# 34 more tiles of gathered rows issued by ScalarE, in one stream of 20 rows a step, with a smaller descriptor store

## Chip, cores and metric

One core of a Trainium2 chip. The metric is device time in microseconds (us) of one execution of the whole kernel; before the change the median of three runs is 10925.68 us (10925.35 to 10929.42).

## What is computed

A recommendation model in fp32, for 16384 users with 69 items each and one label item. The table `emb` has 100001 rows of 96 numbers; the rows are gathered by index, which is most of what the kernel has to move.

```python
u = emb[batch_user]                       # 16384 x 69 x 96
ql = emb[batch_label[:, 0]]               # 16384 x 96
q = jnp.broadcast_to(ql[:, None, :], u.shape)
z = jnp.concatenate([q, u, q - u, q * u], axis=-1)
h = _dice(z @ W1 + b1, a1, EPS_DICE)      # 64 wide
att = (h @ W2 + b2) @ W3 + b3
eff = (batch_user < ITEM_NUM)[..., None]
pre = jnp.where(eff, u * att, 0.0)
pooled = jnp.einsum('gf,bfe->bge', window, pre).reshape(u.shape[0], G * E)
x = jnp.concatenate([pooled, ql], axis=-1)
h = _dice(_bn_eval(x @ Wf1 + bf1, EPS_BN), af1, EPS_DICE)
h = _dice(_bn_eval(h @ Wf2 + bf2, EPS_BN), af2, EPS_DICE)
return h @ Wf3 + bf3
```

`_dice(x, alpha)` is `(alpha * (1 - p) + p) * x` with `p` the sigmoid of the scaled `x`.

## The kernel before

The users are cut into 32 blocks of 512 (`NBLK`, `BLK`). The 512 x 69 rows of a block are 69 chunks (`NCH`) of 512 rows, and a chunk is four tiles (slots 0 to 3) of 128 rows, a row on each partition. The 64 first items of the users make 64 "main" chunks, in which a chunk holds 8 users; the other five items are "tail" chunks of 512 users. Two chunks are a pair, and there are 32 x 69 / 2 = 1104 pairs (`NPAIR`). 1104 x 8 = 8832 tiles of rows are needed, and 128 more for the labels.

There are three ways by which a tile gets into SBUF:

- **GpSimd (POOL)** issues one indirect DMA for a tile: `gather`, line 266 in the trace. It reads 128 indices from `ids` and fetches 128 rows of 384 bytes into the pair's buffer `u` (pool `upool`, 14 buffers, each holding a pair's eight tiles), or into `q` for labels.
- **SyncE (SP)** issues 128 single DMAs of one row each (line 301) for slot 3 of the chunks in `SP_CHUNKS`: the second chunk of every tenth pair, 109 tiles. Its buffers are the first four tiles of `ring`.
- **ScalarE (ACT)** does the same for slot 3 of the chunks in `ACT_CHUNKS`: the first chunk of every eighth pair, 136 tiles, in the next three tiles of `ring`.

For single rows the engine needs each row's place in a register. `Singles.load` (line 286) fetches 32 offsets from the tile `offsets` to registers with one load instruction; then every row is a register move and a DMA issue. Offsets are row numbers times 384, made once at the start by two DVE operations. A tile of rows counts as here when its semaphore reaches 16 x 128; PE waits for that before it transposes the tile (`wait_for_single`).

The order of the work on each engine is written out by hand (`tc.manual_schedule`): `plan` is a list of work for each step, a step for each pair, and the engines' queues get their instructions in that order. In step i stand, in this order: the attention logits of four pairs every fourth step (`attend_rows`: PE `prow`, then the ScalarE copy `row`), the tail chunks of pair i-3, the logits' spreading (`spread`), the hidden layer of pair i-2 (`hidden`: PE `ph`, then on ScalarE the sigmoid of line 405 and the scaling of line 406, then DVE's product `y`), ScalarE's rows of this step (`scalar_rows`), the pooling of pair i-7 (`pool`: PE `acc`, the last use of that pair's tiles in `u` or `ring`), and the fetch of pair i (`fetch`: eight gathers or fewer on POOL, eight transposes `ptr` on PE, two copies and two products on DVE). Every 34.5 steps a block's label rows, its `As` rows (ScalarE copies of `pc`, line 349) and its top layers (lines 483 and 484 on ScalarE) come in between.

ScalarE's rows of one tile are spread over eight steps, 16 rows in each (`ACT_ROWS`, `ACT_STEPS`): tile s is fetched in steps 8s+1 to 8s+8 and used in pair 8s+11. POOL's queue holds nothing but gathers; before the first gather of a pair it waits until the pair 14 before has been pooled. [...]

Of the kernel before, what the change touches and what calls it, by code (L numbers as in the profile page):

```python
# [18 lines left out]
P = 128  # L19
# [31 lines left out]
SLOT = 3  # L51
SP_CHUNKS = [2 * (10 * s + 8) + 1 for s in range(109)]
SP_RING = 4
ACT_CHUNKS = [2 * (8 * s + 11) for s in range(136)]
ACT_RING = 3
ACT_ROWS = 16
ACT_STEPS = -(-P // ACT_ROWS)
SINGLES = SP_CHUNKS + ACT_CHUNKS
NSB = (len(SINGLES) + P - 1) // P
NSEM = 8  # L60


def chunk_of(c):
# [52 lines left out]
def rec_kernel(  # L116
# [12 lines left out]
    nc = tc.nc  # L129
# [1 line left out]

    const = ctx.enter_context(tc.tile_pool(name="const", bufs=1))
    ipool = ctx.enter_context(tc.tile_pool(name="ipool", bufs=2))
    upool = ctx.enter_context(tc.tile_pool(name="upool", bufs=14))
    tpool = ctx.enter_context(tc.tile_pool(name="tpool", bufs=4))
    ypool = ctx.enter_context(tc.tile_pool(name="ypool", bufs=6))
    rpool = ctx.enter_context(tc.tile_pool(name="rpool", bufs=2))
# [137 lines left out]
    class Singles:  # L275

        def __init__(self, name, engine, kind, chunks, first, buffers, group):
            self.name, self.engine, self.kind, self.group = name, engine, kind, group
            self.chunks, self.first, self.buffers = chunks, first, buffers
            self.sems = [tc.alloc_semaphore(f"{name}{k}") for k in range(NSEM)]  # L280
            self.given = [0] * NSEM

# [12 lines left out]
        def fetch(self, s, start, stop):  # L295

            b, k = self.buffers[s % len(self.buffers)], s % NSEM
            for r in range(start, stop):
# [299 lines left out]
    for s, m in enumerate(SP_CHUNKS):  # L598
        at(max(0, m // 2 - 6), lambda s=s: by_sync.fetch(s, 0, P))

    by_scalar = Singles(
        "act",
        nc.scalar,
        mybir.EngineType.Activation,
        ACT_CHUNKS,
        len(SP_CHUNKS),
        range(SP_RING, SP_RING + ACT_RING),
        2 * ACT_ROWS,
    )
    turn = {}  # L610
    for s, m in enumerate(ACT_CHUNKS):
        for k in range(ACT_STEPS):
            turn.setdefault(m // 2 - 2 - ACT_STEPS + k, []).append((s, k * ACT_ROWS, min(P, (k + 1) * ACT_ROWS)))

    def scalar_rows(i):

        for s, start, stop in turn.get(i, []):
            by_scalar.fetch(s, start, stop)

    c = NPAIR - CLOSE  # L620
    for i in range(c):
        if i >= 3 and (i - 3) % 4 == 3:
            at(i, rows_of(i - 6, 4))
        if i >= 3:
            at(i, tails_of(i - 3))
        if i >= 4 and (i - 4) % 4 == 3:
            at(i, spread_of(i - 7, 4))
        if i >= 2:
            at(i, hidden_of(i - 2))
        at(i, lambda i=i: scalar_rows(i))  # L630
        if i < c - CLOSE:
            if i >= POOL_LAG:
                at(i, pool_of(i - POOL_LAG))
        else:

            for k in {0: (-15, -14), 1: (-13,), 3: (-12, -11), 4: (-10, -9), 7: (-8, -7)}.get(i - c + 8, ()):
                at(i, pool_of(c + k))
        at(i, fetch_of(i))
# [116 lines left out]
```

## Time and profile before

| | us |
|---|---|
| median of three runs | 10925.68 |
| the profiled execution | 10926.71 |
| its span, first to last instruction | 10924.9 |
| PE busy (matmuls, their ends modelled) | 8862.0 |
| POOL busy | 8226.3 |
| DVE busy | 4285.5 |
| ScalarE busy, without DMA issue and loads | 1897.5 |
| share of the 16 DMA engines taken by the gathers' queue | 18.7% |

Granted PE clock: 0.745 of full speed in the mean.

How to read it: a line of the groups ("L266 POOL ...") has the line of the code, the engine, the operation, what it writes and reads, how often; behind the bar the busy time of all, the mean of one in ns, then how long the engine stood idle just before them and what ended most of it. "issue" is idle time that ended without the profile showing anything waited for. `ACTq` and `SPq` are the sequencers of ScalarE and SyncE, which issue DMAs and loads; that time is not counted as busy time of the engine. The queue that counts is the one whose idle time nobody else ends.

### The profile page before, as it was taken

How to read it: one execution, taken by the hardware profiler on the slowest of the kernel's cores; microseconds unless marked ns; L12 is line 12 of the kernel's file. 1: busy time of each engine (PE TensorE's matmuls, PEld its weight loads, DVE VectorE, ACT ScalarE, POOL GpSimd, SP SyncE). 2: the span in 40 equal slices, each digit the busy share in tenths (PEclk: the TensorE clock that was granted, in tenths of full speed). 3: DMA queues.
4: the chain of work that ended last, by engine and by line, in shares of the span. 5: the costliest groups of instructions: out<-in, count | busy, mean ns of one | idle time of the engine just before them, and what ended most of it. 6: DMA issues, size and time to landing. Idle time of an engine off the chain costs nothing.

```text
span 10924.9 us, 172203 instructions
## 1 busy us (share of the span) xinstructions
PE 8862.0 (81%) x41797; PEld 4319.5 (40%) x41797; DVE 4285.5 (39%) x7535; ACT 1897.5 (17%) x2761; POOL 8226.3 (75%) x8721
## 2 busy tenths in 40 slices
PE   7878878788887888888878778878888887888878
PEld 3333434343333344333433333334343333433335
DVE  4334333333333333433333333333333333333334
ACT  1111111111111111111111111111111111111112
POOL 7777777777777777777777777777777777777776
PEclk7767777777777777767777777777777777777777
DMA  2212211121111212212111121112212112122111
GB/s 49 42 42 44 42 42 41 42 44 42 42 42 42 44 41 42 42 41 44 42 42 41 42 44 42 42 42 42 44 42 42 42 41 44 42 42 41 42 41 36
DMA packets 344467, 458.51 MB, mean 42 GB/s; under 512 B 202354, under 2 KB 202866, under 8 KB 343330
## 3 DMA queue, kind: packets, MB, share of 16 engines
q0 software_dynamic: 278880, 428.92, 18.7%
q1 hardware_dynamic: 29762, 11.82, 0.5%
q10 hardware_dynamic: 34816, 6.75, 0.4%
q8 instruction: 336, 5.51, 0.2%
q14 instruction: 673, 5.51, 0.2%
HBM read 446.74 MB, written 0.07 MB: 41 GB/s over the span
## 4 chain that ended last, share of the span: by engine, by line
POOL 49%; issue 21%; PE 17%; DMA 12%; DVE 0%; ACT 0%; ACTq 0%; POOLq 0%; DVEq 0%
POOL u L266 48%; DMA u<-in_rows,ids 12%; PE p L502 4%; PE acc L325 4%; PE ph L399 3%; PE ph L403 2%; PE ptr L325 2%; POOL q L266 1%; PE prow L414 1%; PE pa L423 1%; PE ph L396 0%; PE ph L401 0%; PE pc L348 0%; PE patt L431 0%; ACTq L301 0%
## 5 line engine op out<-in xcount | busy, mean ns | idle before, releaser
L266 POOL DMA_INDIRECT u<-in_rows,ids x8587 | 8104.3, 944 | 2620.1 <-issue 2428.2
L325 PE MATMUL ptr<-ident,u 128*96 128x128 f32 x8587 | 2002.8, 332 | 1940.1 <-DMA u<-in_rows,ids 1892.9
L407 DVE TENSOR_TENSOR y<-ph,y 128x512 f32<-128x512 f32 x1104 | 763.5, 692 | 4377.1 <-ACT y L406 4119.6
L325 PEld LDWEIGHTS ptr<-ident,u 128*96 128x96 f32 x8587 | 1139.7, 149 | 2701.4 <-DMA u<-in_rows,ids 2262.6
L325 PEld LDWEIGHTS acc<-rw,u 128*96 128x96 f32 x15930 | 1677.0, 187 | 1204.3 <-issue 977.6
L376 DVE COPY uT<-ptr 96x512 f32<-96x512 f32 x2208 | 1494.1, 677 | 1488.6 <-PE ptr L325 1485.2
L325 PE MATMUL acc<-rw,u 128*96 128x20 f32 x15930 | 1792.5, 258 | 57.8 <-DVE rw L436 41.7
L405 ACT ACTIVATE y<-ph 128x512 f32<-128x512 f32 x1104 | 658.6, 597 | 6308.6 <-PE ph L403 5822.7
L399 PE MATMUL ph<-uT,A 128*64 128x512 f32 x4096 | 1649.8, 883 | 0.0
L403 PE MATMUL ph<-quT,wn 96*64 96x512 f32 x4416 | 1585.2, 788 | 0.0
L379 DVE TENSOR_TENSOR quT<-ptr,qT 96x512 f32<-96x512 f32 x2048 | 1380.2, 674 | 0.0
L406 ACT ACTIVATE y<-y,wn,na1c 128x512 f32<-128x512 f32 x1104 | 898.1, 813 | 36.6
L403 PEld LDWEIGHTS ph<-quT,wn 96*64 96x64 f32 x4416 | 440.7, 188 | 1041.5 <-issue 1040.8
L502 PE MATMUL p<-pooled,wf 96*100 96x512 f32 (+1 forms) x1400 | 693.1, 644 | 0.0
L399 PEld LDWEIGHTS ph<-uT,A 128*64 128x64 f32 x4096 | 264.1, 175 | 616.2 <-issue 608.8
L416 ACT COPY row<-prow 128x512 f32<-128x512 f32 (+1 forms) x277 | 161.6, 583 | 1791.9 <-PE prow L414 1179.1
L470 DVE COPY pooled<-acc 96x160 f32<-96x160 f32 x1008 | 419.9, 417 | 117.6 <-PE acc L325 116.9
L414 PE MATMUL prow<-y,v 128*32 128x512 f32 x2208 | 453.6, 891 | 1.4 <-DVE y L407 1.1
L502 PE MATMUL p<-pre,V 96*100 96x512 f32 (+1 forms) x700 | 394.9, 710 | 3.0 <-DVE x L485 2.7
L502 PEld LDWEIGHTS p<-pooled,wf 96*100 96x100 f32 x1400 | 259.5, 198 | 332.6 <-issue 332.6
L436 DVE SCALAR_TENSOR_TENSOR rw<-patt,bb,wn 128x320 f32<-128x320 f32 x554 | 276.2, 539 | 143.6 <-PE patt L431 142.9
L431 PE MATMUL patt<-ident,row 128*128 128x128 f32 x1108 | 224.9, 340 | 25.1 <-DVE pre L424 22.7
(72 smaller groups left out, 2445.8 us busy)
## 6 DMA issues: line engine op xcount, KB each, us to landing
ring<-in_rows ACTq DMA_DIRECT2D x17408, 0.4 KB
ring<-in_rows SPq DMA_DIRECT2D x13952, 0.4 KB
u<-in_rows,ids POOLq DMA_INDIRECT x8587
ids<-in_idx SPq DMA_DIRECT2D x8, 560.0 KB, 3.9
q<-in_emb,ids POOLq DMA_INDIRECT x128
wf<-in_far SPq DMA_DIRECT2D x1, 1209.0 KB, 6.4
wn<-in_near SPq DMA_DIRECT2D x1, 236.0 KB, 2.8
ids<-in_idx SPq DMA_DIRECT2D x1, 140.0 KB, 2.3
```

What stands on the lines that cost most here:

```text
L266: nc.gpsimd.indirect_dma_start(out=dst, out_offset=None, in_=table, in_offset=bass.IndirectOffsetOnAxis(ap=index, axis=0),)
L325: ins = op(out, ring[:, at[0]].bitcast(F32) if at else u[:, 4 * (c % 2) + t, :], other, **how)
L376: nc.vector.tensor_copy(uT[j][0:E], ptr)
L379: nc.vector.tensor_tensor(quT[:, j, :].rearrange("e (s f) -> e s f", f=FM), ptr.rearrange("e (s f) -> e s f", f=FM), by_field(q[:, k * NS ...
L399: nc.tensor.matmul(p, As[n % 2][:, k // 4, :], uT[j], start=True, stop=False)
L403: nc.tensor.matmul(p, Wp, quT[:, j, :], start=False, stop=True)
L405: nc.scalar.activation(y, ph, AF.Sigmoid, scale=S_DICE)
L406: nc.scalar.activation(y, y, AF.Identity, bias=a1c, scale=na1c)
L407: nc.vector.tensor_mul(y, ph, y)
L414: nc.tensor.matmul(pr[32 * k : 32 * (k + 1), :], v2, ys[b + k], start=True, stop=True)
L470: nc.vector.tensor_copy(pooled[n][:, :, k * NS : (k + 2) * NS].rearrange("e g s -> e s g"), pa.rearrange("e j s g -> e (j s) g"),)
L502: nc.tensor.matmul(p1, w[:, h * DH : (h + 1) * DH], x, start=(k == 0), stop=(k == KTOP - 1))
```

## The change

ScalarE gets 170 tiles for 136, so POOL gathers 34 fewer; SyncE's tiles are the same. ScalarE's rows are one stream: step i issues rows 20i to 20i+19 of all its tiles one after the other, across the tiles' borders, until 170 x 128 = 21760 rows are through (1088 steps). Tile s is used in pair (s+1) x 128 // 20 + 2, about every 6.4 pairs. A load still brings 32 offsets; it stands where the stream comes to a row whose number in the tile divides by 32, so it can fall between the rows of a step. `ring` has four tiles for ScalarE instead of three, `upool` 16 buffers instead of 14, and the store of the gathers' descriptors gets 4096 bytes of each partition. The tile `offsets` grows from two to three columns of 128 (279 tiles in all for 245).

```diff
-ACT_CHUNKS = [2 * (8 * s + 11) for s in range(136)]
-ACT_RING = 3
-ACT_ROWS = 16
-ACT_STEPS = -(-P // ACT_ROWS)
+ACT_ROWS = 20
+ACT_CHUNKS = [2 * ((s + 1) * P // ACT_ROWS + 2) for s in range(170)]
+ACT_RING = 4
...
+RING_BYTES = 4096
...
-    upool = ctx.enter_context(tc.tile_pool(name="upool", bufs=14))
+    upool = ctx.enter_context(tc.tile_pool(name="upool", bufs=16))
...
         range(SP_RING, SP_RING + ACT_RING),
-        2 * ACT_ROWS,
+        32,
     )
-    turn = {}
-    for s, m in enumerate(ACT_CHUNKS):
-        for k in range(ACT_STEPS):
-            turn.setdefault(m // 2 - 2 - ACT_STEPS + k, []).append((s, k * ACT_ROWS, min(P, (k + 1) * ACT_ROWS)))
-
     def scalar_rows(i):
 
-        for s, start, stop in turn.get(i, []):
-            by_scalar.fetch(s, start, stop)
+        row, stop = i * ACT_ROWS, min((i + 1) * ACT_ROWS, len(ACT_CHUNKS) * P)
+        while row < stop:
+            s, start = divmod(row, P)
+            n = min(P - start, stop - row)
+            by_scalar.fetch(s, start, start + n)
+            row += n
...
-    nc = bacc.Bacc("TRN2", target_bir_lowering=False, num_devices=1)
+    nc = bacc.Bacc("TRN2", target_bir_lowering=False, num_devices=1, dynamic_dma_scratch_size=RING_BYTES)
```

## The prediction

> **What bounds the kernel now.** I read the page's groups first, then the waits of POOL, then the chain of waits in a stretch of the middle, last ScalarE's timeline. The page says who works and how often:
>
> ```profile
> span 10924.9 us, 172203 instructions
> PE 8862.0 (81%) x41797; PEld 4319.5 (40%) x41797; DVE 4285.5 (39%) x7535; ACT 1897.5 (17%) x2761; POOL 8226.3 (75%) x8721
> ...
> L266 POOL DMA_INDIRECT u<-in_rows,ids x8587 | 8104.3, 944 | 2620.1 <-issue 2428.2
> L325 PE MATMUL ptr<-ident,u 128*96 128x128 f32 x8587 | 2002.8, 332 | 1940.1 <-DMA u<-in_rows,ids 1892.9
> ...
> ring<-in_rows ACTq DMA_DIRECT2D x17408, 0.4 KB
> ring<-in_rows SPq DMA_DIRECT2D x13952, 0.4 KB
> ```
>
> PE has the larger busy share, but before the transposes it sits 1892.9 us, and what ends that wait is the landing of a gather. POOL looks three-quarters busy, but its idle time ends in "issue", so it waits for nobody. The waits of POOL (total us, times, longest):
>
> ```profile
> POOL u L266 <- issue: 2428.2, 7958, 0.3
> POOL u L266 <- DMA u<-in_rows,ids: 111.1, 364, 0.3
> POOL u L266 <- PE ptr L325: 59.8, 196, 0.3
> POOL q L266 <- issue: 38.7, 127, 0.3
> ```
>
> No entry is longer than 0.3 us, whoever is named: that is the gap after every gather, not a stall. The chain in one stretch shows the pace:
>
> ```profile
> 4001.85 0.94 POOL u L266
> 4002.79 0.30 issue
> 4003.09 0.94 POOL u L266
> 4004.04 0.31 issue
> 4004.34 2.46 DMA u<-in_rows,ids
> ```
>
> A gather starts every 0.94 + 0.30 us; from a gather's start to its landing 2.46 us pass. Over the 8715 gathers (8587 u, 128 q) the mean distance of two starts is 1.249 us. The first starts at 3.3 us and the last ends at 10887.7: 3.3 + 8715 x 1.249 (10884.4) + 37.2 of tail = 10924.9, the whole span. POOL is the bound from start to end, and one gather is worth 1.249 us. PE is on its heels: its last transposition of a pair ends, in the median, 3.0 us after the start of the pair's last gather.
>
> **The change, part by part.**
>
> *Gathers removed.* The instruction lists of the two programs have 8587 and 8553 u gathers, 128 q gathers each. 34 x 1.249 = 42.5 us off POOL. All 34 lie before the last dozen pairs, so the first start and the tail's own work stay.
>
> *ScalarE's extra work.* 34 x 128 = 4352 row DMAs and 136 loads more. What a step of ScalarE looks like now:
>
> ```profile
> 5019.15 0.60 ACT L405 ACTIVATE y<-ph 128x512 f32<-128x512 f32 x1 [10.71 <-PE ph L403]
> 5019.77 0.81 ACT L406 ACTIVATE y<-y,wn,na1c 128x512 f32<-128x512 f32 x1
> 5022.06 5.15 ACTq L301 DMA_DIRECT2D ring<-in_rows  x16
> 5027.31 0.60 ACT L405 ACTIVATE y<-ph 128x512 f32<-128x512 f32 x1 [6.72 <-issue]
> 5027.94 0.81 ACT L406 ACTIVATE y<-y,wn,na1c 128x512 f32<-128x512 f32 x1
> 5028.01 4.99 ACTq L301 DMA_DIRECT2D ring<-in_rows  x16
> ```
>
> The DMA issues are not in the page's 17%. The 2.2 us between the second activation and the first row in the first step are the load of offsets:
>
> ```profile
> L286 ACTq TENSOR_LOAD <-offsets x544: 2132/2182/2236, 16.1 to 10735.1; - x182
> ```
>
> Start to start, two rows lie 0.322 us apart in the mean over all neighbouring rows (0.316 when SyncE issues none, 0.329 beside SyncE's). From above, everything added: 1897.5 + 17408 x 0.322 (5605) + 544 x 2.18 (1187) = 8690 us before, and 8690 + 4352 x 0.322 (1401) + 136 x 2.18 (297) = 10388 after, 95.5% of 10883. From below: summing in the trace the time in which ScalarE's queue stood before an activation or copy gives 2971 us, so it was occupied 7954 us (the L406 activation runs beside the first rows, 898 us in all); 7954 + 1698 = 9652, 88.7%. In steps (1104 pairs): 8.7 to 9.4 us on ScalarE against 8681 x 1.249 / 1104 = 9.82 us on POOL. I take the lower, since the overlap is seen in the lines above (the rows start at 5028.01, the activation ends at 5028.75). ScalarE is behind POOL, but close, so I cost it at nothing on the path and name the cover: behind a burst of rows stand the next step's `row` copy and sigmoid, for which DVE's product and PE's `prow` wait. When they are late, PE is late, and POOL notices only if a gather buffer is not released. In the trace a pair's first gather starts 41.4 us or more (median 60) after PE has pooled the pair that held its buffer; two buffers more add two steps, 19.6 us. ScalarE may thus be four steps behind at its worst before it costs anything. Uncovered, a step's 4 more rows and its share of the loads are 1.6 us (1698 in all).
>
> *Rows arriving in time.* The last row of a tile is now issued two steps before use instead of three. In the trace, from the sigmoid of step i to the slot-3 transposition of step i+2, 21.6 us pass in the median, 13.0 at the 1st percentile, 9.4 at the least. The chain needs 0.6 for the sigmoid, 2.2 for a load, 16 x 0.322 = 5.2 for up to 16 rows and some 2 to land (a gather takes 2.46): 10 us. Late in under 1 of 100 tiles, by about a microsecond, inside the cover above: nothing.
>
> *The smaller descriptor store.* No row of the trace shows a full store. Lower end: nothing, or a little gain never seen. Upper end: the store holds one gather, and each waits for the landing before it: 2.46 instead of 1.249, for 8681 gathers 10.5 ms. In the trace the packets of all but the last one or two gathers are done when a gather starts (median 1 in flight, never over 3), and after the first hundred gathers no distance of two starts exceeds 1.280 us; whatever bookkeeping a turn of the store needs is below 0.03 us. I take nothing, because two gathers in flight suffice (2 x 1.249 > 2.46) and the page's 278880 packets in queue 0 are only 32 per gather.
> [...]
>
> *Does taking transfers to another queue help at all?* The row: POOL's time is 0.94 + 0.30 of issue per gather, while queue 0 keeps the 16 DMA engines 18.7% busy; gathers beside three or four ScalarE rows follow each other in 1248.9 ns, beside none in 1248.5, so rows do not slow them (0.4 ns x 8681 = 3.5 us at most). [...]
>
> *SyncE, the longer offsets tile (384 columns for 256), the group size written as 32* (it was 2 x 16) cost nothing: the tile's two DVE operations stand at the start, where POOL waits for the ids alone; SyncE spends 48.9 us on 127 rows of a 98 us period.
>
> **Sum.** 10924.9 - 42.5 = 10882.4 span. The profiled execution took 10926.7, 1.8 more than its span, and the median of the runs shown is 10925.7: forecast 10925.7 - 42.5 = 10883.2.
>
> **Rivals.**
> 1. *ScalarE becomes the bound.* Upper count with the spacing beside SyncE: 1897.5 + 680 x 2.18 + 21760 x 0.329 = 10539, and the waits for `prow`, `pc` and the top layers' sums, which a full queue cannot fill (371 us of the 2971): 10910, within 0.2% of before. For it: ScalarE is at 88 to 96%. Against: the overlap of L406, and 9.82 us a step on POOL. It decides where rows are over 0.345 us apart by the upper count, 0.379 by the lower.
> 2. *PE is the bound at once, the gathers hidden anyway:* 10925, no change. Against: 1892.9 us of waiting for gathers, in all slices alike.
> 3. *Slower: the store runs full.* Place: POOL, ahead of each gather. Price: with one gather in it 8681 x 2.46 = 21.4 ms; it decides as soon as fewer than two fit, and 4.9 ns more per gather (42.5 / 8681) already eat the gain. For it: the store is a quarter, and its accounting is not visible. Against: at most 3 in flight.
> That the change is not what it says is excluded by the lists: 8553 gathers, 21760 rows, 680 loads on ScalarE.
>
> **How the numbers follow.** Forecast 0.80, ScalarE 0.08, PE 0.03, store 0.07, the rest 0.02. Below the forecast: the first hundred gathers' irregular starts may go (2.6 us), one gather's place before the tail (1.2), a run's spread (0.4): 10879. Above: 3.5 for pace, 3.7 for the spread of the three runs, 6.4 if one burst of 20 rows lengthens the tail: 10897. A measurement here tells 0.2% (22 us) from no change. Faster 0.83: the forecast and a milder ScalarE; same 0.07; slower 0.10.
>
> **What would show it.** Right: u gathers 8553 times at 944 ns with waits of 0.3 us at most, the last ending near 10845; ScalarE's queue standing some 1230 us (2971 - 1698 - 42) instead of 2971; PE's wait for gathers smaller by tens of us. Wrong: any POOL wait over 0.3 us (on a DMA: the store; on PE's `acc`: buffers, so ScalarE or PE), a gather mean above 949 ns, or PE waiting for `row` or `y`.

## The result and the profile after

The changed kernel takes 10888.85 us in the median of seven runs (10887.48 to 10891.12), the kernel before 10925.35 (10924.22 to 10929.42, seven runs too): 36.5 us less, ratio 0.9965 with a 95% interval from 0.9956 to 0.9975. The forecast was 10883.2 with a range of 10879 to 10897. The two profiled executions, 10926.71 and 10887.48, lie 39.2 us apart.

The page of the changed kernel:

```profile
span 10885.7 us, 181041 instructions
PE 8803.6 (81%) x41797; PEld 4302.5 (40%) x41797; DVE 4246.3 (39%) x7535; ACT 1888.2 (17%) x2761; POOL 8195.5 (75%) x8687
...
L266 POOL DMA_INDIRECT u<-in_rows,ids x8553 | 8073.8, 944 | 2610.2 <-issue 2420.3
L325 PE MATMUL ptr<-ident,u 128*96 128x128 f32 x8553 | 1958.2, 331 | 1759.2 <-DMA u<-in_rows,ids 1708.8
...
ring<-in_rows ACTq DMA_DIRECT2D x21760, 0.4 KB
```

34 gathers fewer, each still 944 ns, and the idle time before them still ends in "issue". POOL's waits (total us, times, longest):

```profile
POOL u L266 <- issue: 2420.3, 7931, 0.3
POOL u L266 <- DMA u<-in_rows,ids: 91.0, 298, 0.3
POOL u L266 <- PE ptr L325: 68.4, 224, 0.3
```

Nothing over 0.3 us: POOL is still the bound from the first gather to the last. The last gather ends at 10847.0 us instead of 10887.7, 40.7 us earlier, and the tail behind it is 38.8 us instead of 37.2. ScalarE looks different. Its timeline, in the same stretch as in the prediction:

```profile
5006.85 0.60 ACT L405 ACTIVATE y<-ph 128x512 f32<-128x512 f32 x1 [8.53 <-issue]
5007.48 0.81 ACT L406 ACTIVATE y<-y,wn,na1c 128x512 f32<-128x512 f32 x1
5007.55 8.84 ACTq L301 DMA_DIRECT2D ring<-in_rows  x20
5016.43 1.06 ACT L349 COPY A<-pc 32x512 f32<-32x512 f32 x2 [8.13 <-issue]
5017.82 0.60 ACT L405 ACTIVATE y<-ph 128x512 f32<-128x512 f32 x1 [0.33 <-PE ph L403]
5018.45 0.81 ACT L406 ACTIVATE y<-y,wn,na1c 128x512 f32<-128x512 f32 x1
5018.52 6.50 ACTq L301 DMA_DIRECT2D ring<-in_rows  x20
```

20 rows take 6.50 us; where a load of offsets falls among them, 8.84. The work behind (the copies at 5016.43) starts as soon as the last row is issued and its wait ends in "issue": PE had been done before. Summed over the trace, ScalarE's queue stands still 1185 us; it was 2971. What this does to PE shows in PE's waits, here the changed kernel's:

```profile
PE ptr L325 <- DMA u<-in_rows,ids: 1708.8, 2059, 2.4
PE acc L325 <- DVE rw L436: 134.6, 72, 7.4
PE prow L414 <- DVE y L407: 47.7, 18, 4.8
```

Before, these three were 1892.9, 41.7 and 1.1 us; the second of them then:

```profile
PE acc L325 <- DVE rw L436: 41.7, 39, 4.0
```

PE now waits 140 us more for what hangs on ScalarE's late activations and copies, and 184 us less for gathers: it comes later to transposes whose rows have landed in the meantime. PE's last transposition of a pair ends 3.4 us (median) after the pair's last gather started, and 8.8 us at the 95th percentile, where it was 3.0 and 4.9.

### The profile page after: what moved, and what is told of

Its sections match the earlier page's. It is cut to its first block, busy times and chain, and to the rows that moved or that the text cites. A ratio compares the mean times of both kernels' runs of the same rounds, so it can differ in the third digit from the quotient of the medians.

```text
span 10885.7 us, 181041 instructions
## 1 busy us (share of the span) xinstructions
PE 8803.6 (81%) x41797; PEld 4302.5 (40%) x41797; DVE 4246.3 (39%) x7535; ACT 1888.2 (17%) x2761; POOL 8195.5 (75%) x8687
## 4 chain that ended last, share of the span: by engine, by line
POOL 46%; issue 21%; PE 19%; DMA 10%; ACTq 2%; ACT 1%; DVE 1%; POOLq 0%
POOL u L266 45%; DMA u<-in_rows,ids 10%; PE p L502 4%; PE acc L325 4%; PE ph L399 3%; PE ph L403 3%; PE ptr L325 2%; ACTq L301 2%; PE prow L414 1%; POOL q L266 1%; PE pa L423 1%; PE ph L396 1%; ACTq L286 1%; PE ph L401 1%; PE pc L348 0%
## 5 line engine op out<-in xcount | busy, mean ns | idle before, releaser
L325 PE MATMUL ptr<-ident,u 128*96 128x128 f32 x8553 | 1958.2, 331 | 1759.2 <-DMA u<-in_rows,ids 1708.8
L399 PE MATMUL ph<-uT,A 128*64 128x512 f32 x4096 | 1613.0, 863 | 0.0
L414 PE MATMUL prow<-y,v 128*32 128x512 f32 x2208 | 498.6, 894 | 52.6 <-DVE y L407 47.7
L485 DVE SCALAR_TENSOR_TENSOR x<-p,wf,g 100x512 f32<-100x512 f32 (+3 forms) x105 | 73.9, 704 | 506.1 <-ACT g L484 502.2
```

The source lines that it names most:

```text
L325: ins = op(out, ring[:, at[0]].bitcast(F32) if at else u[:, 4 * (c % 2) + t, :], other, **how)
L399: nc.tensor.matmul(p, As[n % 2][:, k // 4, :], uT[j], start=True, stop=False)
L414: nc.tensor.matmul(pr[32 * k : 32 * (k + 1), :], v2, ys[b + k], start=True, stop=True)
```

## The experiments

The experiments ran on several chips, and the times of the same kernel differ. Over the gathers after the first hundred, one starts every 1.2487 us (before) and 1.2490 (changed) in the traces of the first comparison, and every 1.2506 to 1.2515 in the later traces in which POOL is the bound; the kernel before takes 10943 and 10948 us there, in the median. What sets this pace is open, and it need not be the chip: one of the 15 executions of the kernel before on the chip of the first four experiments took 10925.07, as in the first comparison, and on that same chip a gather takes 943.9 ns in the trace with 24 rows and 945.7 in the one with the store of 14336 bytes. On two other chips the kernel before takes 13632 and 13616 us; of that below. So each time stands beside the kernel before on its own chip, and expectations given as absolute times are read as differences.

**The store alone.** The kernel before, with

```diff
-    nc = bacc.Bacc("TRN2", target_bir_lowering=False, num_devices=1)
+    nc = bacc.Bacc("TRN2", target_bir_lowering=False, num_devices=1, dynamic_dma_scratch_size=4096)
```

> The kernel before with nothing changed but the descriptor store of 4096 bytes. Theory (of the 6 us that the forecast was off, the store has some: in the changed kernel's trace every 28.4th start of a gather comes about 9 ns late, and 8715 / 28.4 = 306 turns are 2.7 us): 2 to 4 us longer than before, gathers' mean distance after the first hundred 1.2489 to 1.2490 us instead of 1.2487, the period of 28.4 in it, the tail after the last gather 37 us as before. Rival (the store costs nothing, ScalarE's lateness is all of the 6 us): within 1 us of before. Rival (the store runs full at times): waits of POOL over 0.3 us.

Measured: 10945.12 us against 10943.17, 2.0 us more; the ratio, 1.0002 (0.9993 to 1.0011), can't tell that from no change, but the trace can. When the gathers' starts are sorted by their place in a period of 28.44 gathers (4096 / 28.44 = 144 bytes for each), the one at the turn of the period comes 8.6 ns later than the others: 306 turns x 8.6 ns = 2.6 us. The old store, whose size the kernel before doesn't name, has turns, too: sorted by a period of 113.8, four times as long, the trace of the kernel before shows 8.7 ns at 76 turns, 0.7 us; at 144 bytes a gather this would be a store of 16384 bytes. That size, and that the store has been used once through at a turn, are estimates from these periods. So the smaller store costs some 2.0 us more. No POOL wait was over 0.3 us. The store costs its turns, and no wait shows it full.

**The rows without the small store.** The changed kernel with

```diff
-RING_BYTES = 4096
+RING_BYTES = 14336
...
-    upool = ctx.enter_context(tc.tile_pool(name="upool", bufs=16))
+    upool = ctx.enter_context(tc.tile_pool(name="upool", bufs=14))
```

> The changed kernel with a store of 14336 bytes and 14 gather buffers: ScalarE's 170 tiles alone, as near as the memory allows. Theory (one gather is worth 1.249 us, two more buffers nothing, the small store 2 to 4 us): 2 to 4 us below the changed kernel, thus 10885 to 10887; no wait of POOL over 0.3 us; least distance of a gather to the release of its buffer about 33 us (52.5 less two steps). Rival (the buffers matter): slower than the changed kernel, POOL waiting for PE's acc. Rival (the store costs nothing): the changed kernel's time within 1 us.

Measured: 10901.98 against 10943.17, 41.2 us less (ratio 0.9964, 0.9951 to 0.9978). No POOL wait over 0.3 us; the least distance of a pair's first gather to the release of its buffer was 36.4 us, so the two further buffers are not needed. The period of 28.44 is gone (1.3 ns); in its place stands one of 14336 / 144 = 99.6, with 8.7 ns. Against the store alone, on the same chip, the mean distance of gathers is 0.26 ns shorter, 2.3 us over them all. As a difference the expectation comes to 38.5 to 40.5 us; the gain is a little larger. The tail is 39.2 us with this larger store, where the changed kernel had 38.8: that speaks for ScalarE's rows, and against the store, as what makes the tail later.

**More rows on ScalarE.** The changed kernel with

```diff
-ACT_ROWS = 20
-ACT_CHUNKS = [2 * ((s + 1) * P // ACT_ROWS + 2) for s in range(170)]
+ACT_ROWS = 24
+ACT_CHUNKS = [2 * ((s + 1) * P // ACT_ROWS + 2) for s in range(204)]
```

> 24 rows a step, 204 tiles: 34 gathers fewer again, 4352 more rows and 136 loads on ScalarE. Theory (ScalarE's queue, of which 1185 us stood still in the changed kernel, is now over-full): 10886 - 1185 + 4352 x 0.322 + 136 x 2.26 = 11409 us occupied, so the time is 11400 or more, slower than before; POOL waits for PE (buffers) for hundreds of us. Rival (POOL stays the bound): 10889 - 42 = 10847.

Measured: 11703.83 us, ratio 1.0693 (1.0677 to 1.0709) to the kernel before. ScalarE's queue stands still only 339 us. POOL's waits:

```profile
POOL u L266 <- issue: 2291.3, 7509, 0.3
POOL u L266 <- PE ptr L325: 674.7, 301, 11.6
POOL u L266 <- PE acc L325: 248.4, 87, 12.0
```

and PE's, in the same execution:

```profile
PE prow L414 <- DVE y L407: 854.9, 211, 6.8
PE acc L325 <- DVE rw L436: 471.9, 193, 11.3
```

The chain of work that ended last, in shares of the span:

```profile
ACTq 64%; issue 15%; PE 11%; ACT 9%; DVE 1%; DMA 0%; POOL 0%
```

The longest entries are what separates this from the changed kernel: POOL stops up to 12 us for a buffer, because PE stops for `y` and `rw`, which hang on ScalarE, and the chain runs through ScalarE's issues. Four rows more a step turn a gain of some 40 us into a loss of some 760.

**More tiles for SyncE.** The changed kernel with

```diff
-SP_CHUNKS = [2 * (10 * s + 8) + 1 for s in range(109)]
+SP_CHUNKS = [2 * (6 * s + 8) + 1 for s in range(181)]
```

> The changed kernel with SyncE's tiles every 6 pairs instead of every 10: 181 tiles for 109, 72 gathers fewer. Theory (POOL is the bound, SyncE has room: 181 x (128 x 0.33 + 4 x 2.17) = 9217 us): 10889 - 72 x 1.249 = 10799, give or take 5. Rival (the bound passes to PE and ScalarE, which stand still 1185 us less what a wider spacing of rows beside SyncE's takes): the gain less than half of 90 us, 10845 or more, with POOL waiting over 0.3 us for acc.

Measured: 10817.5 against 10943.17, 125.7 us less (ratio 0.9887, 0.9872 to 0.9902). By the first comparison's 36.5, 36.5 + 72 x 1.249 = 126.4 was to be had (the changed kernel itself did not run on this chip). POOL's waits:

```profile
POOL u L266 <- issue: 2353.7, 7709, 0.3
POOL u L266 <- DMA u<-in_rows,ids: 122.4, 401, 0.3
POOL u L266 <- PE ptr L325: 82.5, 270, 0.3
```

POOL is the bound even with 106 gathers fewer than in the kernel before, and a gather moved to SyncE is worth about what one moved to ScalarE is, as long as the queue has room: against the version with the store of 14336 bytes, on the same chip, 84.5 us for 72 gathers, of 90.1 less 2.0 for the store and 1.3 for a tail of 40.5 us; some 2 us stay open. This has the largest gain of all versions tried.

**Four runs on a chip where instructions stall.** The changed kernel again; the changed kernel with `RING_BYTES = 1024`; with `ACT_ROWS = 22` and 187 tiles; and with

```diff
-SP_CHUNKS = [2 * (10 * s + 8) + 1 for s in range(109)]
+SP_CHUNKS = [2 * (11 * s // 2 + 8) + 1 for s in range(197)]
```

> The changed kernel once more, so that all can be compared on one chip. Theory (34 gathers, the store's turns 2 to 3 us, ScalarE's lateness in the tail 1.5 us): 38 to 39 us below the kernel before; the last gather ends 40 us earlier than in the kernel before, the tail is 38 to 40 us where the clock at the end is near 0.9. Rival (something else takes 6 us): 36 us or less below, with a pace above 1.0003 times that of before.

> The changed kernel with a store of 1024 bytes. Theory (a turn of the store costs about 9 ns, whatever its size; the period falls to a quarter of 28.4, 7.1 gathers, 1221 turns): 8 to 9 us more than the changed kernel, gathers' mean distance about 1 ns longer, no wait of POOL over 0.3 us, since at most 3 or 4 gathers are in flight. Rival (the store runs full): some distances over 1.3 us, tens of us or more. Rival (the store is costless): the same time within 1 us.

> 22 rows a step, 187 tiles: 17 gathers fewer, 2176 rows and 68 loads more on ScalarE. Theory (ScalarE's queue becomes the bound when what it is occupied plus what it can never fill reaches POOL's time; 24 rows left 339 us unfilled): occupied 10886 - 1185 + 2176 x 0.322 + 68 x 2.26 = 10555, with 339 it is 10894, against POOL's 10889 - 21 = 10868: both meet, so 10868 to 10900, the gain of 21 us lost in part or whole, POOL waiting over 0.3 us for the first time. Rival (POOL stays the bound as long as ScalarE is under 100%): 10868 give or take 2.

> The changed kernel with a tile of SyncE's every 5.5 pairs, 197 tiles, 88 gathers fewer than the changed kernel. Theory (POOL is the bound; SyncE occupied 197 x (128 x 0.33 + 4 x 2.17) = 10031 of 10780 us): 110 us below the changed kernel. Rival (SyncE is late with its tiles, PE waits for them, the buffers fill): less than the gain of a tile every 6 pairs (90 us below the changed kernel).

Measured: the kernel before 13631.78 us there, these four 14461.17 (ratio 1.0602, 1.0588 to 1.0617), 14589.48, 14948.26 and 16456.22. None of the expectations fits. The changed kernel and the one with the small store ran again, on a second chip of that kind:

> The changed kernel again, since on the chip of the run before both kernels' ScalarE rows lay 0.53 us apart in the mean, not 0.32. Theory (on a chip with rows 0.32 us apart POOL is the bound; 34 gathers less the store's turns and the later tail): 38 to 40 us below the kernel before on this chip. If rows lie over 0.38 us apart again, ScalarE's queue is the bound and the changed kernel is slower than the one before. Rival (something else takes 6 us): 36 us or less below, with rows 0.32 us apart.

> As the run with the store of 1024 bytes, beside the changed kernel on one chip. Theory (each turn of the store costs about 9 ns): 8 to 9 us more than the changed kernel, mean distance of gathers about 1 ns longer with a period of 7.1, no POOL wait over 0.3 us. Rival (the store runs full): some distances over 1.3 us, tens of us or more. Rival (costless): the same within 1 us.

13615.64 us for the kernel before, 14474.06 (1.0616, 1.0597 to 1.0636) and 14599.72. Of the first expectation the second branch held: rows over 0.38 us apart, and the changed kernel slower than the one before. What is different is seen in the trace of the changed kernel on the second of these chips, in the head of its page and its chain:

```profile
span 14498.3 us, 181041 instructions
...
ACTq 47%; issue 30%; PE 13%; ACT 6%; DVE 2%; another core or an unknown queue 1%; POOL 0%; DMA 0%; DVEq 0%; POOLq 0%
ACTq L301 40%; ACTq L286 7%; ACT y L405 4%; PE acc L325 3%; PE ptr L325 2%; PE ph L399 2%; PE ph L403 2%; PE p L502 1%; PE prow L414 1%; ACT y L406 1%; PE pa L423 1%; DVE y L407 0%; PE ph L396 0%; DVE uT L376 0%
```

The chain runs through ScalarE's row issues, POOL has no share of it. The median distance of two rows is 304 ns as elsewhere, but the mean is 529: in bursts, instructions of ScalarE's and SyncE's queues follow each other in steps of about 0.7 us (a register move that takes 29 ns elsewhere takes 700, or the next instruction comes 700 later; one in ten of ScalarE's moves takes so long). ScalarE's timeline shows 17 rows in the window's 10.1 us, where 20 took 6.50:

```profile
5001.22 0.60 ACT L405 ACTIVATE y<-ph 128x512 f32<-128x512 f32 x1 [8.26 <-issue]
5001.85 0.82 ACT L406 ACTIVATE y<-y,wn,na1c 128x512 f32<-128x512 f32 x1
5001.92 10.13 ACTq L301 DMA_DIRECT2D ring<-in_rows  x17
```

With more tiles for SyncE the chain passes to SyncE's queue (the execution with a tile every 5.5 pairs):

```profile
span 16481.6 us, 203916 instructions
...
SPq 62%; issue 36%; PE 1%; ACTq 0%; another core or an unknown queue 0%; DMA 0%; DVE 0%; ACT 0%; DVEq 0%
```

There ScalarE stands still 2697 us, so it isn't a matter of ScalarE alone; SyncE's 25216 rows lie 0.59 us apart in the mean and with its loads fill 16285 of the 16482 us. So in both traces the fuller of the two issuing queues has little time left (ScalarE's stands still some 640 us of the 14498).

On these chips the time also goes with the number of instructions, nearly: 13632 us for 172203 of them, 14461 for 181041, 14948 for 185461, 16456 for 203916, 79.2, 79.9, 80.6 and 80.7 ns each. But almost all the instructions added are row moves, row issues and loads of these same two queues, and each costs more than the mean (87 to 110 ns), so the count of instructions and the fullness of a queue are not told apart. Why these queues are slow there the traces do not tell. The DMAs that bring instructions took no longer than elsewhere (1062 and 428 ns in the mean of the two queues on the second of these chips, 1085 and 431 in the first comparison).

The question of the 1024-byte store could still be read there: among gathers not held up, the one at the turn of 1024 / 144 = 7.1 gathers starts 8.8 ns late, and distances over 1.3 us are no more frequent at a turn (131 of 914, one in 7.0) than elsewhere. So a turn costs the same for a small store, and the starts show no sign that seven gathers' room is too little. But the version with the small store takes 126 to 128 us more than the changed kernel on these two chips, with the same number of instructions, where 8 to 9 were expected; that is not explained. The 22 rows and the tile every 5.5 pairs were not tried on another chip.

**Fewer rows, and the changed kernel once more.** The changed kernel with 12 rows a step,

```diff
-ACT_ROWS = 20
-ACT_CHUNKS = [2 * ((s + 1) * P // ACT_ROWS + 2) for s in range(170)]
+ACT_ROWS = 12
+ACT_CHUNKS = [2 * ((s + 1) * P // ACT_ROWS + 2) for s in range(102)]
```

> The changed kernel with 12 rows a step, 102 tiles on ScalarE: 34 gathers more than the kernel before, 4352 rows and 136 loads fewer. Theory where rows lie 0.32 us apart: POOL is the bound, 8749 gathers, 34 x 1.249 = 42.5 us more than the kernel before, 2 to 3 us more for the store's turns, so 44 to 46 us slower than before. Theory where rows lie 0.5 us apart (there the time went with the number of instructions, 79 to 81 ns for each, 172203 before and 181041 changed): 163365 x 0.0795 = 12990, some 640 us faster than the kernel before on that chip. Rival there (only ScalarE's own queue is slow and bounds): faster, too, but SyncE's further tiles would then have cost nothing, and 88 of them cost 1995 us.

and beside it the changed kernel:

> The changed kernel again. Theory where rows lie 0.32 us apart: 34 gathers (42.5), less 2 to 3 us for the store's turns, less 1.5 us for the later tail: 38 to 40 us below the kernel before on this chip. Rival: 36 us or less below, so that 2 to 3 us more have another cause. Where rows lie 0.5 us apart: 181041 x 0.0800 = 14480.

The rows lay 0.32 us apart on this chip. Before 10947.9; 12 rows 10991.66 (ratio 1.0041, 1.0026 to 1.0056), 43.8 us more, just under the 44 to 46 expected; 20 rows 10910.32 (0.9967, 0.9955 to 0.9979), 37.6 us less. Between the two lie 68 gathers, 68 x 1.2515 = 85.1 us, and 81.3 were measured. The last gathers end 83.7 us apart and the tails are 36.0 and 37.9 us: 1.9 us of the shortfall is the tail. So each step of 34 gathers brings its full price but for one or two microseconds, and between these two traces the tail is later with more rows on ScalarE. The changed kernel's 37.6 us lie between theory (38 to 40) and rival (36 or less).

## Why the prediction was right, and where its sizes were off

*POOL is the bound and one gather is worth 1.249 us.* Right: no POOL wait over 0.3 us after the change, gathers of 944 ns, and with 12, 16 and 20 rows a step and with SyncE's 72 tiles more the time followed the number of gathers, on the chips where rows lie 0.32 us apart.

*The term that was mis-sized is what stands behind POOL's 42.5 us: two costs taken as nothing.* The store: "whatever bookkeeping a turn of the store needs is below 0.03 us. I take nothing". It is 8.6 ns for each of 305 turns, 2.6 us, less the 0.7 us of the old store's turns: 2.0 us. The mean distance of gathers after the first hundred rose by 0.30 ns, 2.6 us over them all; the 0.6 us beyond the turns are open. ScalarE's lateness: "I cost it at nothing on the path", covered by the gather buffers. That cover holds in the middle (least distance 52.5 us with 16 buffers). At the end there are no further gathers, and PE's lag is the span's: at the last pair its transposes end 5.6 us after the last gather started instead of 4.4, and the tail grew by 1.5 us (37.2 to 38.8), 1.9 between 12 and 20 rows. The range had put 6.4 us there.

The traces suggest where this lag comes from: in pair 1090, just behind ScalarE's last rows, PE's last transposition is 10.8 us behind the last gather, before 2.8, and the pairs that are left don't take all of it back. And the tail follows it: with 12 rows the lag at the last pair is 3.1 us and the tail 36.0, with 20 rows the lags are 4.7, 5.6 and 6.0 and the tails 37.9, 38.8 and 39.2, with SyncE's further tiles 7.7 and 40.5; tail less lag is 32.9 to 33.2 us in all of these and in the kernel before. It is one trace each, and with the store alone (ScalarE's rows as before) the lag is 2.9, so 1.5 us is also what executions differ by: that ScalarE's rows are the cause is argued, not isolated.

Together: 42.5 - 2.6 - 1.5 = 38.4, against 39.2 between the profiled executions, 36.5 and 37.6 between medians; one or two microseconds are not accounted for. Tails can vary by more from one execution to the next: in the profiled one with the store alone, which took 5.9 us more than the median of its kernel, the tail is 42.7 us at a granted clock of 0.72,

```profile
10906.50:10949.00 42.50, 35.96 (x223) 30.40 (x223) 7.81 (x19) 7.84 (x16) 0.06 (x1) 0.72 0.01 3
```

while the kernel before ends at 0.91 (the last numbers of these lines are granted clock, DMA share and GB/s):

```profile
10887.70:10924.00 36.30, 31.62 (x241) 25.13 (x239) 9.70 (x24) 9.03 (x18) 0.00 (x1) 0.91 0.02 4
```

*ScalarE's occupation.* Between 9652 and 10388 us were forecast and the lower end was taken; it was 10886 - 1185 = 9701. The loads more than account for the 49 us over it: the 136 that still stand behind an activation take 2.17 us as before, the 544 that now stand between rows take 2.29, some 60 us more in all.

*Rows in time.* Right: the least time from a tile's last row issue to its transposition is 11.6 us, where a gather took 2.46 to land.

*The store's room.* The period with which a gather starts late went with the store's size: 28.44 gathers for 4096 bytes, 7.1 for 1024 and 99.6 for 14336, 144 bytes a gather each time; before the change it was 113.8, four times 28.44. The rival in which the store runs full did not occur with the period at a quarter of that (no POOL wait over 0.3 us); at a sixteenth the starts show no sign of it, with the 126 us open. Taking gathers to another queue did help: a gather's start was its price (0.94 + 0.30 us on POOL), and 34 tiles moved were worth 36.5 us.

*The first rival, ScalarE as the bound,* had the right condition in kind, though no run lay near its threshold: it decides "where rows are over 0.345 us apart by the upper count, 0.379 by the lower". With 24 rows 0.32 us apart the queue was over-full by count and the kernel 7% slower; on the two chips with rows 0.53 us apart on average the changed kernel itself is 6% slower than the one before, with ScalarE's queue in the chain. The prediction did not consider that the spacing of rows could differ from chip to chip. That the first comparison ran where rows lie 0.32 us apart is luck, as far as the prediction goes: it gave this rival 0.08, and on two of the chips used here it is what happens.

## What to carry to other kernels

Price a move between queues by the queue that it leaves, and ask of the queue that receives it how much of its time is spoken for by all its instructions, issues and loads included, not by the engine's busy share: 17% stood on the page and 89% were occupied. Look for where lateness is covered: in the first comparison POOL never waited over 0.3 us for PE in the changed kernel, while gather buffers stood free 52.5 us ahead or more, but at the end, with no gather left, the tail was 38.8 us instead of 37.2. A gain that rests on filling a queue of many short instructions to nine tenths is bought with its margin, and is worth a look on more than one chip: the ratio was 0.9965 in the first comparison and 0.9967 on the chip with the 12 rows, 1.0602 and 1.0616 on two others.

## What the hardware showed that was not expected

The same program ran at 10925 to 10948 us on some chips and at 13616 to 13632 us on two others, where stretches of ScalarE's and SyncE's instructions come in steps of about 0.7 us and five programs of 172203 to 203916 instructions took 79 to 81 ns for each. Where POOL is the bound, gathers start 1.2487 to 1.2515 us apart in the mean, from one trace to another. That is 0.2%, more than half of what this change brings, and the cause is open. A turn of the descriptor store costs 8.4 to 9.0 ns, whether it comes every 7 gathers or every 114.
